# Eight PSUM banks, shared out anew: scores, transposes and products in a sliding-window attention block

## The chip, the cores and the metric

The kernel runs on one core of one Trainium2 chip, in one launch. The metric is the device time of that launch in microseconds. The engines are called by their short names: PE (TensorE, matmuls; PEld are its weight loads), DVE (VectorE), ACT (ScalarE), POOL (GpSimd) and SP (which here only starts DMAs). PSUM, into which PE writes, has eight banks of 128 x 512 floats; each PSUM tile of this kernel takes one bank.

## What is computed

A block with three residual steps on `x` of shape (8, 512, 512), float32: eight batch rows of 512 tokens. First and third come feed-forward steps, in the middle attention:

```python
x = x + 0.5 * ffn(layernorm(x), w_gate_up, w_proj)
x = x + attention(layernorm(x), Wq, Wk, Wv, Wo)
x = x + 0.5 * ffn(layernorm(x), w_gate_up, w_proj)
```

The attention has 32 heads of 16 values. A token sees itself and the 128 tokens before it, so a block of 128 queries needs its own block of keys and the previous one. Scores are `q k / 4`, then softmax, then the weighted sum of the values, then the output product with `Wo`. The feed-forward step has ternary weights, a gated SiLU and an RMS norm.

## The kernel before, in words

There are three stages: feed-forward "a", attention "b", feed-forward "c". Rows go between them through DRAM (`rows_a`, `rows_b`). The pools of a stage are laid out over the PSUM banks in the order in which they are opened, so attention reuses the banks of stage "a", and stage "c" those of attention. Stage "a" has its four accumulators first (`ps_acc`), then two gate-up banks (`ps_mm`), then two for transposes (`ps_tr`). Stage "c" opens its two transpose banks first, then four accumulators, then two gate-up banks.

In attention the work is cut into 128 **units** `u`. A head group `i = u // 4` holds eight of the 32 heads of one batch row (`i = 4 b + j`), and `t = u % 4` is the block of 128 tokens. In the text, `g` counts the four pairs of heads in a group; PE works on the four pairs side by side, each in 32 of its rows. For every unit there are:

- `maxima(u)` (L480, L489): scores with queries on the partitions, four tiles `sm`, one for each `g`. DVE masks each and takes its maximum into `negs`. It runs six units ahead (`AHEAD`).
- `subtract(i)` (L498, L501): after the four units of a head group, `negs` is transposed (`neg`) and the maxima are added into the queries as an extra component.
- `probabilities(u)` (L512 to L532): scores again with keys on the partitions, four tiles `sp`. ACT reads tiles g = 0, 2 and 3 (L525), DVE tile g = 1 (L521), both into `pT`; ACT then takes the exponential (L527), and POOL cuts off what lies outside the window (L532).
- `weighted(u)` (L548): values times `pT`, into `av`. After every second unit ACT copies it to `ab` (L557).
- `turned(u)` (L566): transposes `ab` into `abT`, for every second unit. `divided(u)` (L572, L576): DVE divides by the sum of the weights. `turned_back(u)` (L588, L591): transposes the result back, tile `oTp`, and ACT copies it to `oT`.

Between them lie the products with full-size matrices, one in each unit of a head group: values `wv` at t = 0 (read out by DVE), output `wo` of the previous row at t = 1 (DVE), queries `wq` at t = 2 (ACT, two copies), keys `wk` at t = 3 (ACT). All go through `sum_of_products` (L426). In the third head group of a row the layer norm of a later row is worked in: DVE scales (`xn_b`, L197), PE transposes (`ptn_b`, L205), ACT copies to `xs_b` (L213).

The order on PE, DVE, ACT and POOL inside this stage is the order in which the loop at the end of `attention_stage` calls these functions; the scheduler doesn't change it. It does merge that order with the instructions of the stages before and after. The first units have negative numbers: there row 0's norm (at high priority), the first products and the first maxima run. Units from 128 on (`units`) do what is left over, the output products of row 7 among them. A PSUM tile can be written as soon as its bank's last tile has been read out, and each engine works strictly in its order, so a tile without a bank holds up all of PE behind it.

Of the kernel before, what the change touches and what calls it, by code (L numbers as in the profile page):

```python
# [8 lines left out]
F32 = mybir.dt.float32  # L9
# [6 lines left out]
P = 128  # L16
# [8 lines left out]
def macaron_block(  # L25
# [20 lines left out]
    B, T, D = x.shape  # L46
    FF = w_proj.shape[1]
    TB, DC, FC = T // P, D // P, FF // P
# [50 lines left out]
    PSUM = bass.MemoryType.PSUM  # L99

    def pool(stack, name, bufs, space=bass.MemoryType.SB):

        return stack.enter_context(
            tc.tile_pool(name=name, bufs=bufs, space=space, reuse_waits="tile")
        )
# [64 lines left out]
    def inv_sqrt(dst, src):  # L170
        nc.gpsimd.tensor_tensor(dst, src, mhalf, ALU.pow)

    def norm(xnpool, xspool, psum, tag, xt, split, name):

        if split:
            xs = xspool.tile([P, 2, DC, T], F32R, tag="xs", name=f"xs_{name}")
        else:
            xs = xspool.tile([P, DC, T], F32, tag="xs", name=f"xs_{name}")  # L180
        mv = small.tile([P, TB, 2], F32, tag="mv", name=f"mv_{name}")
        rstd = small.tile([P, TB], F32, tag="nrstd", name=f"rstd_{name}")

        def statistics(t):
            st = small.tile([P, 6], F32, tag="st", name=f"st_{name}_{t}")
            nc.vector.bn_stats(st, xt[:, t, :])
            nc.vector.bn_aggr(mv[:, t, :], st)
            if t == TB - 1:
                var = small.tile([P, TB], F32, tag="nvar", name=f"var_{name}")
                nc.vector.tensor_scalar(var, mv[:, :, 1], LN_EPS, None, ALU.add)  # L190
                inv_sqrt(rstd, var)

        xns = {}

        def scaled(t):
            xns[t] = xnpool.tile([P, D], F32, tag="xn", name=f"xn_{name}_{t}")
            nc.vector.tensor_scalar(  # L197
                xns[t], xt[:, t, :], mv[:, t, 0:1], rstd[:, t : t + 1], ALU.subtract, ALU.mult
            )

        def transposed(t):
            xn = xns.pop(t)
            pt = psum.tile([P, DC, P], F32, tag=tag, name=f"ptn_{name}_{t}")
            for c in range(DC):
                nc.tensor.transpose(pt[:, c, :], xn[:, c * P : (c + 1) * P], ident)  # L205
            cols = slice(t * P, (t + 1) * P)
            if split:
                nc.scalar.copy(xs[:, 0, :, cols], pt)
                nc.vector.tensor_tensor(
                    xs[:, 1, :, cols], pt, xs[:, 0, :, cols].bitcast(F32), ALU.subtract  # L210
                )
            else:
                nc.scalar.copy(xs[:, :, cols], pt)  # L213

        return xs, statistics, scaled, transposed
# [155 lines left out]
    def attention_stage():  # L371
# [5 lines left out]
        s = ExitStack()  # L377
        xpool = pool(s, "x_b", 2)
        xspool = pool(s, "xs_b", 2)
        xnpool = pool(s, "xn_b", 2)  # L380
# [5 lines left out]
        probs = pool(s, "probs_b", 3)  # L386
        opool = pool(s, "o_b", 8)
        work = pool(s, "work_b", 3)
        ps_s = pool(s, "ps_s", 5, PSUM)
        ps_av = pool(s, "ps_av", 1, PSUM)  # L390
        ps_mm = pool(s, "ps_mm_b", 2, PSUM)

        xss, norms = {}, {}

        def row_loaded(b):
            xt = xpool.tile([P, TB, D], F32, tag="x", name=f"x_b{b}")
            nc.sync.dma_start(xt, rows_a[b])
            xss[b], *norms[b] = norm(xnpool, xspool, ps_mm, "mm", xt, False, f"b{b}")

        row_loaded(0)  # L400
        attn_w = {}
# [14 lines left out]
        abTs, qs, ks, kz, pTs, avs, abs_, os_, oTs = {}, {}, {}, {}, {}, {}, {}, {}, {}  # L416
        NJ = DC
        units = B * NJ * TB
# [2 lines left out]
            return u // TB // NJ, u // TB % NJ, u % TB  # L421

        def sum_of_products(name, pairs, done):
            ps = ps_mm.tile([P, T], F32, tag="mm", name=name)
            for n, (lhs, rhs) in enumerate(pairs):
                nc.tensor.matmul(ps, lhs, rhs, start=(n == 0), stop=(n == len(pairs) - 1))  # L426
            done(ps)
# [23 lines left out]
        def keys_of_head(i, h, kept, at):  # L451
            kz[i][h] = ring.tile([P, T], F32, tag=f"kz{h}", name=f"kz{h}_{i}")
            nc.gpsimd.tensor_scalar(kz[i][h], ks[i], kept, at, ALU.mult, ALU.add)
# [39 lines left out]
                    )  # L493

        def subtract(i):
            pt = ps_mm.tile([P, TB, P], F32, tag="mm", name=f"neg_{i}")
            for t in range(TB):
                nc.tensor.transpose(pt[:, t, :], negs[i % 2][:, t, :], ident)  # L498
            flat = pt.rearrange("p t q -> p (t q)")
            for h, at in enumerate((at16, at0)):  # L500
                nc.vector.scalar_tensor_tensor(qs[i][h], flat, at, qs[i][h], ALU.mult, ALU.add)  # L501
# [57 lines left out]
        def turned(u):  # L559

            i, t = u // TB, u % TB
            pt = abTs[i] = ps_mm.tile([P, 2, 2, P], F32, tag="mm", name=f"abT_{u}")
            ab = abs_.pop(i)
            for m in range(2):
                for h in range(2):
                    nc.tensor.transpose(pt[:, m, h, :], ab[:, h, m, :], ident)  # L566

        def divided(u):
            i, t = u // TB, u % TB
            rows = abTs.pop(i).rearrange("p m h (g r) -> p (m h) g r", r=32)  # L570
            rden = small.tile([P, 4, NG, 1], F32, tag="rden", name=f"rden_{u}")
            nc.vector.reciprocal(rden, rows[:, :, :, DK : DK + 1])  # L572
            os_[i] = work.tile([P, 2, NG, 2, DK], F32, tag="o", name=f"o_{u}", bufs=2)
            for m in range(2):
                for h in range(2):
                    nc.vector.tensor_tensor(  # L576
                        os_[i][:, m, :, h, :], rows[:, 2 * m + h, :, :DK],
                        rden[:, 2 * m + h].to_broadcast([P, NG, DK]), ALU.mult,
                    )

        def turned_back(u):
            i, t = u // TB, u % TB
            if t == 1:
                oTs[i] = opool.tile([P, T], F32, tag="oT", name=f"oT_{i}")
            o = os_.pop(i)
            back = ps_mm.tile([P, 2, P], F32, tag="mm", name=f"oTp_{u}")
            for m in range(2):
                nc.tensor.transpose(  # L588
                    back[:, m, :], o[:, m].rearrange("p g h d -> p (g h d)"), ident
                )  # L590
            nc.scalar.copy(  # L591
                oTs[i][:, (t - 1) * P : (t + 1) * P], back.rearrange("p m q -> p (m q)")
            )
# [23 lines left out]
        for u in range(-row - row // 2 - 2, units + row):  # L617
            i, t = u // TB, u % TB
            b, j = i // NJ, i % NJ
            if b == -2 and j == 2:  # L620
                with tc.high_priority():
                    if t == 0:
                        for block in range(TB):
                            norms[0][0](block)
                    for part in norms[0][1:]:
                        part(t)
            if 0 <= u < units:
                probabilities(u)
            if 0 <= u - 2 < units and (u - 2) % 2 == 1:
                divided(u - 2)  # L630
            if later:
                keys_of_head(*later.pop(0))
            if 0 <= u - 1 < units:
                weighted(u - 1)
            if t == 0 and 0 <= b - 1 < B:
                residual_loaded(b - 1, j)
            if 0 <= u + AHEAD < units:
                maxima(u + AHEAD)
            if j in (1, 2) and 0 < b + 2 < B:
                norms[b + 2][j - 1](t)  # L640

            if 0 <= u - 1 + AHEAD < units and (u - 1 + AHEAD) % TB == TB - 1:
                subtract((u - 1 + AHEAD) // TB)
            if b == -1 and j >= 2 and t < 2:
                values(0, 2 * (j - 2) + t)
            if t == 0 and 0 < b + 1 < B:
                values(b + 1, j)
            if t == 1 and 0 <= b - 1 < B:
                output(b - 1, j)
            if t == 2 and 0 <= i + 3 < B * NJ:  # L650
                queries(i + 3)
            if t == 3 and 0 <= i + 3 < B * NJ:
                keys(i + 3)
            if j == 2 and 0 < b + 2 < B:
                norms[b + 2][2](t)
            if 0 <= u - 1 < units and (u - 1) % 2 == 1:
                turned(u - 1)
            if 0 <= u - 2 < units and (u - 2) % 2 == 1:
                turned_back(u - 2)
            if j == 0 and t == 3 and 0 < b + 2 < B:  # L660
                row_loaded(b + 2)
# [33 lines left out]
```

## Time and profile before

| | us |
|---|---|
| median of 3 runs | 2562.67 (2561.23 to 2563.18) |
| profiled execution, its own time | 2563.55 |
| its span in the profile | 2561.5 |
| PE busy in the span | 2452.0 (96%) |
| DVE busy | 1310.7 (51%) |
| ACT busy | 977.0 (38%) |
| POOL busy | 948.5 (37%) |
| attention on PE, first `wq` to last `wo`, about | 831 to 1828 |
| PE, 1500 to 1600 us | busy 98.22 of 100 |

The page of the profile gives busy time by engine, then the chain of work that ended last, then the costliest groups of instructions. A timeline line reads: start, length, engine, line, operation, output <- inputs, sizes, how many, and in brackets how long the engine was idle before, and who ended the wait. Two things need care. A group's length on PE runs to the modelled end of its last matmul, which lies after the start of what follows; the time from start to start is the surer measure. And a group of matmuls that is held up in its middle counts as busy.

### The profile page before, as it was taken

Reading aid. Unit: us, or ns where it says so; the run is one execution under the profiler, and the core shown is the slowest. Engines: PE = TensorE matmul, PEld = TensorE weight load, DVE = VectorE, ACT = ScalarE, POOL = GpSimd, SP = SyncE. Lnnn points to the kernel's source line nnn. Section 1 sums busy time; section 2 is a strip of 40 time slices with the busy share of each in tenths; the row PEclk is TensorE's granted clock in tenths of the full one; section 3 lists DMA queues with packets and bytes.
Section 4 is the critical chain, followed back from the end, with each engine's and each line's share of the span. In section 5 each row is a group of like instructions: output and inputs, shape, how many; then the busy total and the mean of one; then the engine's idle time right before and its main releaser. Section 6 shows DMA issues by size and latency. Waiting matters only on the chain.

```text
span 2561.5 us, 40354 instructions
## 1 busy us (share of the span) xinstructions
PE 2452.0 (96%) x16184; PEld 1792.2 (70%) x16184; DVE 1310.7 (51%) x3785; ACT 977.0 (38%) x1460; POOL 948.5 (37%) x806
## 2 busy tenths in 40 slices
PE   5789999999999999999999999998999999999998
PEld 4668888888887555555555555555688888888887
DVE  7774434433434565666666565665334434443432
ACT  6662222222222355555555555555322222222221
POOL 0004444444445132333332332333244444444444
PEclk9899999999999999999999999999999999999999
DMA  4430000000011000101010000012400000000000
GB/s 156 140 132 33 34 17 17 33 33 1 34 66 66 34 1 28 36 18 34 22 34 18 18 22 18 19 62 105 144 1 33 33 33 1 34 33 1 34 17 17
DMA packets 38908, 103.26 MB, mean 40 GB/s; under 512 B 2880, under 2 KB 6976, under 8 KB 35648
## 3 DMA queue, kind: packets, MB, share of 16 engines
q1 hardware_dynamic: 28736, 75.51, 8.3%
q10 hardware_dynamic: 9984, 25.17, 2.9%
q8 instruction: 127, 2.08, 0.3%
q14 instruction: 61, 0.50, 0.1%
HBM read 62.91 MB, written 37.75 MB: 39 GB/s over the span
## 4 chain that ended last, share of the span: by engine, by line
PE 88%; DVE 7%; ACT 3%; issue 1%; DMA 1%; POOL 0%; DVEq 0%; POOLq 0%; ACTq 0%; SPq 0%
PE gu_a L233 18%; PE gu_c L233 18%; PE o_c L266 8%; PE o_a L266 8%; PE sm L480 6%; PE sp L512 5%; PE wk L426 5%; PE av L548 4%; PE wq L426 4%; PE wo L426 4%; PE wv L426 4%; PE abT L566 1%; DVE seen L489 1%; PE neg L498 1%; PE oTp L588 1%
## 5 line engine op out<-in xcount | busy, mean ns | idle before, releaser
L233 PE MATMUL gu_a<-xs_a,wgu_a 128*128 128x512 f32 x2048 | 506.9, 400 | 15.2 <-ACT wgu_a L153 15.2
L233 PE MATMUL gu_c<-xs_c,wgu_c 128*128 128x512 f32 x2048 | 488.8, 391 | 0.2 <-ACT sg_c L239 0.2
L532 POOL TENSOR_SCALAR_AFFINE_SELECT pT<-pT 128x1024 f32<-128x1024 f32 x224 | 241.7, 1099 | 630.3 <-ACT pT L527 629.3
L233 PEld LDWEIGHTS gu_a<-xs_a,wgu_a 128*128 128x128 f32 x2048 | 391.1, 193 | 98.9 <-ACT wgu_a L153 17.6
L233 PEld LDWEIGHTS gu_c<-xs_c,wgu_c 128*128 128x128 f32 x2048 | 382.9, 188 | 79.3 <-ACT sg_c L239 0.6
L489 DVE CUSTOM_DVE_ANT_0 seen<-sm,window 128x256 f32<-128x256 f32 (+1 forms) x1024 | 331.6, 388 | 107.5 <-PE sm L480 106.5
L266 PE MATMUL o_a<-wp_a,hs_a 128*128 128x512 f32 x1024 | 253.9, 391 | 5.9 <-ACT wp_a L153 5.9
L266 PE MATMUL o_c<-wp_c,hs_c 128*128 128x512 f32 x1024 | 251.5, 389 | 0.0
L259 POOL TENSOR_TENSOR sq_c<-h_c 128x512 f32<-128x512 f32 x120 | 125.0, 1042 | 323.0 <-DVE h_c L241 308.2
L241 DVE TENSOR_TENSOR h_c<-gu_c,sg_c 128x512 f32<-128x512 f32 x128 | 88.4, 691 | 292.4 <-PE gu_c L233 290.9
L525 ACT ACTIVATE pT<-sp 128x512 f32<-128x512 f32 (+1 forms) x384 | 181.1, 545 | 149.1 <-PE sp L512 148.5
L266 PEld LDWEIGHTS o_a<-wp_a,hs_a 128*128 128x128 f32 x1024 | 191.0, 188 | 46.8 <-ACT wp_a L153 7.8
L241 DVE TENSOR_TENSOR h_a<-gu_a,sg_a 128x512 f32<-128x512 f32 x128 | 88.4, 691 | 257.8 <-PE gu_a L233 256.4
L527 ACT ACTIVATE pT<-pT 128x2048 f32<-128x2048 f32 (+1 forms) x128 | 217.2, 1697 | 7.9 <-DVE var_c L190 2.1
L266 PEld LDWEIGHTS o_c<-wp_c,hs_c 128*128 128x128 f32 x1024 | 192.2, 188 | 39.9
L259 POOL TENSOR_TENSOR sq_a<-h_a 128x512 f32<-128x512 f32 x105 | 109.9, 1046 | 276.2 <-DVE h_a L241 264.8
L260 POOL TENSOR_TENSOR ss_c<-ss_c,sq_c 128x512 f32<-128x512 f32 x120 | 191.8, 1598 | 8.9
L521 DVE TENSOR_SCALAR pT<-sp 128x512 f32<-128x512 f32 (+1 forms) x128 | 80.0, 625 | 210.6 <-PE sp L512 202.1
L239 ACT ACTIVATE sg_c<-gu_c 128x512 f32<-128x512 f32 x128 | 76.7, 599 | 268.8 <-PE gu_c L233 268.8
L243 ACT CAST hs_c<-h_c 128x512 fp32r<-128x512 f32 x128 | 79.5, 621 | 257.0 <-DVE h_c L241 257.0
L239 ACT ACTIVATE sg_a<-gu_a 128x512 f32<-128x512 f32 x128 | 76.7, 599 | 258.3 <-PE gu_a L233 258.3
L480 PE MATMUL sm<-k,q 32*128 32x256 f32 (+1 forms) x2048 | 171.1, 380 | 3.2 <-DVE pT L521 1.6
(128 smaller groups left out, 3076.0 us busy)
## 6 DMA issues: line engine op xcount, KB each, us to landing
x_a<-x_dram SPq DMA_DIRECT2D x8, 1024.0 KB, 5.4
wf_gu<-w_gate_up_dram SPq DMA_DIRECT2D x16, 512.0 KB, 3.7
wgu_kept<-wgu_a SPq DMA_DIRECT2D x16, 512.0 KB, 2.8
rows_a<-x_a ACTq DMA_DIRECT2D x8, 1024.0 KB, 3.9
x_b<-rows_a SPq DMA_DIRECT2D x8, 1024.0 KB, 4.9
xr<-rows_a ACTq DMA_DIRECT2D x32, 256.0 KB, 3.1
rows_b<-xr SPq DMA_DIRECT2D x32, 256.0 KB, 2.4
x_c<-rows_b SPq DMA_DIRECT2D x8, 1024.0 KB, 4.8
```

Source lines behind the costliest of these rows:

```text
L233: nc.tensor.matmul(ps, wgu[c][:, i * DC + k, :], xs[:, s, k, :], start=(k == 0 and s == 0), stop=(k == DC - 1 and s == 1),)
L239: nc.scalar.activation(sg, gu[0], AF.Silu)
L241: nc.vector.tensor_tensor(h, gu[1], sg, ALU.mult)
L259: nc.gpsimd.tensor_tensor(sq, h, h, ALU.mult)
L260: nc.gpsimd.tensor_tensor(sumsq, sumsq, sq, ALU.add)
L266: nc.tensor.matmul(ops[t], ht[:, s, t * P : (t + 1) * P], wp[e // 2][:, e % 2, :], start=(e == 0 and s == 0), stop=(e == FC - 1 and s == 1),)
L426: nc.tensor.matmul(ps, lhs, rhs, start=(n == 0), stop=(n == len(pairs) - 1))
L480: nc.tensor.matmul(tiles[g][:, h, : n * P], qs[i][h][r, t * P : (t + 1) * P], ks[i][r, at], start=True, stop=True,)
L489: nc.vector.tensor_tensor_reduce(out=seen[:, : n * P], in0=tiles[g][:, h, : n * P], in1=window[:, (2 - n) * P :], scale=-1.0, scalar=3.4e3 ...
L525: nc.scalar.activation(under, tiles[g][:, :, : n * P], AF.Relu, scale=-1.0)
L527: nc.scalar.activation(seen, seen, AF.Exp, scale=-1.0)
L532: nc.gpsimd.affine_select(out=half, in_=half, compare_op=ALU.is_ge, fill=0.0, base=0, pattern=[[0, 2 * NG], [sign, P]], channel_multiplier ...
```

## The change

The score pool grows from five buffers to six. The product pool shrinks from two to one. The transposes (`ptn_b`, `neg`, `abT`, `oTp`) no longer use the product pool; they take buffers of the score pool, under its tag, in turn with the scores. The products take the one product buffer while `0 <= u < 128`, and score buffers before and after that. The division of a pair of units is called at the end of the unit that turned it, in place of the next unit, after that unit's `probabilities`. Nothing is computed otherwise.

```diff
-        ps_s = pool(s, "ps_s", 5, PSUM)
+        ps_s = pool(s, "ps_s", 6, PSUM)
         ps_av = pool(s, "ps_av", 1, PSUM)
-        ps_mm = pool(s, "ps_mm_b", 2, PSUM)
+        ps_mm = pool(s, "ps_mm_b", 1, PSUM)
...
-            xss[b], *norms[b] = norm(xnpool, xspool, ps_mm, "mm", xt, False, f"b{b}")
+            xss[b], *norms[b] = norm(xnpool, xspool, ps_s, "s", xt, False, f"b{b}")
...
         def sum_of_products(name, pairs, done):
-            ps = ps_mm.tile([P, T], F32, tag="mm", name=name)
+            space, tag = (ps_mm, "mm") if 0 <= u < units else (ps_s, "s")
+            ps = space.tile([P, T], F32, tag=tag, name=name)
...
         def subtract(i):
-            pt = ps_mm.tile([P, TB, P], F32, tag="mm", name=f"neg_{i}")
+            pt = ps_s.tile([P, TB, P], F32, tag="s", name=f"neg_{i}")
...
-            pt = abTs[i] = ps_mm.tile([P, 2, 2, P], F32, tag="mm", name=f"abT_{u}")
+            pt = abTs[i] = ps_s.tile([P, 2, 2, P], F32, tag="s", name=f"abT_{u}")
...
-            back = ps_mm.tile([P, 2, P], F32, tag="mm", name=f"oTp_{u}")
+            back = ps_s.tile([P, 2, P], F32, tag="s", name=f"oTp_{u}")
...
             if 0 <= u < units:
                 probabilities(u)
-            if 0 <= u - 2 < units and (u - 2) % 2 == 1:
-                divided(u - 2)
...
             if 0 <= u - 1 < units and (u - 1) % 2 == 1:
                 turned(u - 1)
+                divided(u - 1)
```

## The prediction

> **What bounds the kernel now.** I read the page first: busy time by engine, then the chain that ended last.
>
> ```profile
> PE 2452.0 (96%) x16184; PEld 1792.2 (70%) x16184; DVE 1310.7 (51%) x3785; ACT 977.0 (38%) x1460; POOL 948.5 (37%) x806
> PE 88%; DVE 7%; ACT 3%; issue 1%; DMA 1%; POOL 0%; DVEq 0%; POOLq 0%; ACTq 0%; SPq 0%
> ```
>
> TensorE is the bound, and the two feed-forward stages, untouched but for their borders, take all but about 980 us (831 to 1813). Inside attention, the view of waits (TensorE and its weight loads, 900 to 1780 us) looks harmless:
>
> ```profile
> PE abT L566 <- ACT ab L557: 6.8, 4, 1.8
> PE sm L480 <- DVE pT L521: 1.6, 1, 1.6
> PEld sm L480 <- DVE pT L521: 10.3, 44, 1.8
> ```
>
> The third line is the hint: the weight load of the score matmuls waits 44 times for an eviction. It hides in "busy" time, because some of the four matmul groups are already running. The timeline of TensorE shows it. One head group `i` is four units (t = 0 to 3):
>
> ```profile
> 998.76 1.15 PE L512 MATMUL sp<-q,kz 32*128 32x256 f32 x16
> 999.84 0.64 PE L548 MATMUL av<-pT,vones_sb 128*32 128x128 f32 x16
> 1000.41 1.83 PE L480 MATMUL sm<-k,q 32*128 32x256 f32 x16
> 1002.18 3.70 PE L426 MATMUL wo<-wo_sb,oT 128*128 128x512 f32 x8
> ...
> 1008.11 0.98 PE L480 MATMUL sm<-k,q 32*128 32x128 f32 x16
> 1009.02 0.66 PE L498 MATMUL neg<-ident,negs 128*128 128x128 f32 x4
> ...
> 1015.15 1.15 PE L480 MATMUL sm<-k,q 32*128 32x256 f32 x16
> 1016.23 3.70 PE L426 MATMUL wk<-xs_b,wk_sb 128*128 128x512 f32 x8
> ...
> 1022.16 1.40 PE L480 MATMUL sm<-k,q 32*128 32x256 f32 x16
> 1023.49 3.70 PE L426 MATMUL wv<-wv_sb,xs_b 128*128 128x512 f32 x8
> ```
>
> Start to start, `sm` takes 1.08 us at t=3, but 1.77 at t=1 and 1.33 at t=0. The half-width `sm` at t=2 takes 0.91, against 0.65 for a half-width `sp` (1013.49 to 1014.14). So 0.69 + 0.25 + 0.26 = **1.20 us of hidden stall** per `i`; a period is 28.80 us (994.69 to 1023.49). What `sm` waits for is in the all-engine timeline:
>
> ```profile
> 999.98 1.57 ACT L525 ACTIVATE pT<-sp 128x512 f32<-128x512 f32 x3 [3.49 <-PE sp L512]
> 1000.07 0.69 DVE L521 TENSOR_SCALAR pT<-sp 128x512 f32<-128x512 f32 x1 [0.94 <-PE sp L512]
> 1000.68 0.25 DVE L572 RECIPROCAL rden<-abT 128x16 f32<-128x16 f32 x1
> 1000.96 0.62 DVE L576 TENSOR_TENSOR o<-abT,rden 128x64 f32<-128x64 f32 x4
> ```
>
> With five buffers, the four `sm` tiles take one spare and those of `sp` g0 (ACT, 1000.58), g1 (DVE, 1000.76) and g2 (ACT's second, about 1001.07). The fourth group then needs its 1.07 us: 1001.12 + 1.07 = 1002.19, and `wo` starts at 1002.18. The model of the stall closes.
>
> **What the Trainium skill says.** "Perfetto Trace Analysis", Optimization Strategy: the same gap repeating on the engine that should be saturated can mean too few PSUM buffers. The trace agrees (every `i`). "PSUM — Partial Sum Buffer", Terms: eight banks. 5+1+2 and 6+1+1 both use all eight, so a score buffer is bought with a product buffer. "TensorE: Matmul & The Clock Gate", What's actually happening: after about 3.4 us of idling the array's clock halves until it has been busy about as long. The trace agrees: after 3.86 us idle at 945.5, `sp` took 2.02 us to the next start instead of 1.08, and the following `av` 1.50 instead of 1.01.
>
> **Part by part.** I read slots as a ring: a tile waits for the tile six (was five) before it. I choose this reading because the arithmetic above fits it.
>
> *Six buffers, transposes among them.* In order, an `i` takes: t=0 sp4, sm4, abT; t=1 sp4, sm4, oTp; t=2 sp4, sm4, neg, abT; t=3 sp4, sm4, oTp. Counting back six, `sm` now takes the last `sm` tile's slot, one transpose's slot, and `sp` g0 and g1. It no longer needs g2.
> - t=0: g1 is out at 1022.07, before `sm` starts at 1022.16. The stall of 0.25 goes.
> - t=2: g1 is out at 1007.99, `sm` starts 1008.11. The 0.26 goes.
> - t=1: `av` is only half as long here, so g1 (1000.76 + 0.05) still comes late: end 1000.81 + 1.07 = 1001.88 instead of 1002.18. Gain 0.30; 0.39 stays.
> - t=3: no stall before. After: `neg`'s, `abT`'s, g0's and g1's slots are free by about 1015.1 against a need from 1015.15 on. Nothing.
>
> Sum 0.81 per `i`. `sp` needs tiles of the previous unit's `sm`, read out by 1004.7 for a start at 1006.03: hidden. What is late next is g1's eviction by DVE at t=1.
>
> *The division moves.* The same five DVE instructions (0.25 + 0.62, about 0.9 us with the gap) now stand ahead of `pT` instead of behind it. `abT` ends 998.76 and DVE is done with `vones` at 999.12, so they fit into 999.14 to 1000.04, while DVE waits for `sp` until 1000.07: cost nothing, and `abT`'s slot is free 1.5 us earlier than today. At t=2/3 `abT` ends 1013.49, division to 1014.6, `pT` to 1015.0, needed at 1015.35: covered. Without that cover, g1 would be later by the whole 0.9.
>
> *One product buffer.* Each product must be read out before the next begins. wv: out 999.12, wo starts 1002.18. wo: 1006.60, wq 1009.52. wq: two ACT copies (0.69 + 0.68) to 1014.42, wk 1016.23. wk: 1020.56, wv 1023.49. The least slack is 1.8 us: cost nothing.
>
> *Norm transposes off the product buffers.* In the six rows with them, abT at t=2 waits for wq's copies through its buffer ("0.92 <-ACT q L440" at 1314.15), oTp at t=3 for wk's (0.24 shown, 0.3 by starts). Both go: 1.3 us. But at t=0 and t=1 `ptn_b` waits for DVE's `xn_b`, which follows `seen` and doesn't come earlier: of 0.25 + 0.30 only some 0.2 stays. Net about 0.9 beyond a plain `i`.
>
> *Sum inside.* Rows 1 to 6: 24 × 0.81 = 19.4. Norm extra in rows 1 to 5: 5 × 0.9 = 4.5. Row 0 has no `wo`, and its `sp` at t=2 waits for DVE's maxima: about 0.7 × 4 = 2.8. Row 7 waits at `abT` for ACT (1.6 to 3.1 us each), which swallows t=0 and t=2: 1. Gain **27.7 us**. Bounds: 15 (half of it swallowed by DVE) to 39 (t=1 wholly cured).
>
> *The entry.* Today row 0's four `ptn_b` run at 805.6 in the middle of the last feed-forward row, in banks that it has free; they cost 3.63 us there (16 gate-up matmuls take 801.12 to 808.38, 7.26 instead of 3.63). Now they start in the score buffers, whose first four banks are that stage's accumulators.
>
> ```profile
> 830.16 0.95 PE L274 MATMUL ms_a<-ones,ss_a 128*128 128x1 f32 x8
> 830.97 3.68 PE L426 MATMUL wq<-xs_b,wq_sb 128*128 128x512 f32 x8
> 832.64 2.73 DVE L284 SCALAR_TENSOR_TENSOR x_a<-o_a,half_a,x_a 128x512 f32<-128x512 f32 x4
> ```
>
> They must follow `x_a` (2.2 us after `ms_a` ends, all four by 4.3), then the third and fourth `xn_b` (0.55 each, two buffers), `ptn_b` and ACT's copy (0.6 + 0.6): `wq` starts about 6.7 us after `ms_a` instead of at once. Minus 3.63, minus the 0.35 stall at 842.3, plus 1.7 for a slow clock after that idling: **+4.4**, bounds 0 and +9.
>
> *The exit.* Today `ptn_c` fills a hole from 1806.96 while ACT and POOL finish the last `pT`. Its two banks now hold the last `abT` and the first late `wo` (final reads about 1814.9 and 1817.7). So some 2.5 us of transposes move out of the hole; the last `abT` and `wo` come forward by 1.3. **+1**, bounds −1 and +4. DMAs: none added, and SP's queue keeps its order.
>
> Total −27.7 + 4.4 + 1 = **−22.3**. The profiled execution took 2563.55 us (span 2561.5), 0.88 above the median of 2562.67. 2563.55 − 22.3 = 2541.2, or 2540.4 against the median.
>
> **Rivals.**
> - *As worked out*: 2540, own range 2527 to 2553. 0.76.
> - *DVE is the next gate*: the eviction of g1 and the maxima set the pace, so inside only 15 comes, and the borders cost 9 + 2: 2559, no change. For it: `seen` is 2.8 us per unit, and t=1 already hangs on g1. Against it: DVE is 18 of 28.8 us busy. 0.10, partly faster.
> - *The transposes' slots hold up the scores*: if the division runs after `pT` after all, or DVE is late by as much, `abT`'s slot is freed at 1001.58 instead of 1000.04, and `sm` at t=1 ends at 1001.58 + 0.06 + 1.07 = 1002.71, 0.53 worse than today; likewise t=3. Per `i` +1.05 − 0.51 = +0.54, × 31 + 5.4 = +22: 2585. It decides against the change from about 1001.2 on, that is 1.2 us later than I forecast. Against it: the division is issued ahead of `pT`. 0.10.
> - *The ring isn't a ring*, or the stall is ACT's pace and g1 as late as g2: t=1 gains nothing, −9.3: 2550. 0.04.
>
> **How the numbers follow.** A measurement of this kernel tells about 0.2% (5 us) from no change. Faster by more: the first case nearly whole, the last, some of the second: 0.82. Within: 0.08. Slower: 0.10. The range reaches from 2525 (t=1 wholly cured) to 2560, which takes in the second case and leaves the slow one out.
>
> **What would show it.** `sm` start to start: 1.08 at t=0, about 1.45 at t=1, 0.65 at t=2; period 28.0. Division before `pT` on DVE. "abT <- ACT q" gone. First `wq` about 6.7 us after `ms_a`, `ptn_b` between. Wrong: `sm` at t=1 or t=3 longer than before, a product waiting for `vones`, `q` or `k`, or an entry over 10 us.

## The result, and the profile after

The changed kernel took **2534.21 us** (median of four runs, 2530.88 to 2537.88) against 2562.93 in the runs of the kernel before beside it: ratio **0.989, 95% interval 0.987 to 0.991**. The forecast was 2540.4 with a range of 2525 to 2560. The profiled execution took 2530.88 us (span 2528.8), 32.7 less than the profiled one of before. In the listing of the changed kernel most lines of the attention stage stand two further down (`sm` is L482, `sp` L514, `pT` L523 and L527).

The page of the changed kernel: busy time by engine, then the chain that ended last.

```profile
PE 2421.7 (96%) x16184; PEld 1770.2 (70%) x16184; DVE 1304.7 (52%) x3785; ACT 974.9 (39%) x1460; POOL 946.9 (37%) x806
PE 89%; DVE 6%; ACT 2%; issue 1%; DMA 1%; POOL 0%; DVEq 0%; POOLq 0%; ACTq 0%; SPq 0%
```

PE does the same 16184 matmuls, is as full as before (96%), and is "busy" for 30.3 us less. That is how a stall inside matmul groups looks when it goes: the busy time shrinks, the share stays. The timeline of PE over one plain head group of the changed kernel shows where:

```profile
1333.43 3.70 PE L428 MATMUL wv<-wv_sb,xs_b 128*128 128x512 f32 x8
...
1339.15 1.53 PE L482 MATMUL sm<-k,q 32*128 32x256 f32 x16
1340.61 3.70 PE L428 MATMUL wo<-wo_sb,oT 128*128 128x512 f32 x8
...
1346.54 0.73 PE L482 MATMUL sm<-k,q 32*128 32x128 f32 x16
1347.20 0.66 PE L500 MATMUL neg<-ident,negs 128*128 128x128 f32 x4
...
1360.34 1.15 PE L482 MATMUL sm<-k,q 32*128 32x256 f32 x16
1361.41 1.12 PE L428 MATMUL wv<-wv_sb,xs_b 128*128 128x512 f32 x2
```

Start to start, `sm` takes 1.46 us at t=1 (was 1.77), 0.66 at t=2 (0.91) and 1.07 at t=0 (1.33); from `wv` to `wv` it is 27.98 us instead of 28.80. What is left at t=1 is in the all-engine timeline a head group later:

```profile
1365.76 0.25 DVE L574 RECIPROCAL rden<-abT 128x16 f32<-128x16 f32 x1
1366.04 0.62 DVE L578 TENSOR_TENSOR o<-abT,rden 128x64 f32<-128x64 f32 x4
1366.70 1.57 ACT L527 ACTIVATE pT<-sp 128x512 f32<-128x512 f32 x3 [3.24 <-PE sp L514]
1366.79 0.69 DVE L523 TENSOR_SCALAR pT<-sp 128x512 f32<-128x512 f32 x1
1367.13 1.53 PE L482 MATMUL sm<-k,q 32*128 32x256 f32 x16
1368.59 0.30 PEld L428 LDWEIGHTS wo<-wo_sb,oT 128*128 128x128 f32 x2 [0.33 <-issue]
```

The division now stands ahead of DVE's `pT`, which ends at 1367.48. Add 0.05 for the release and 1.07 for the fourth group, and `wo` starts at 1368.60; it started at 1368.59. The gate has moved from ACT's second tile to DVE's one, as worked out.

**Where the time went.** The span cut at four marks (the last `ms_a`, which ends stage "a" on PE; first `sp`; last `sp`; end), in us. The third row, first to last `sp`, is called "inside" below:

| | before | after | difference |
|---|---|---|---|
| start to last `ms_a` | 830.16 | 822.38 | −7.78 |
| last `ms_a` to first `sp` | 44.90 | 54.55 | +9.65 |
| first `sp` to last `sp` | 930.38 | 889.60 | −40.78 |
| last `sp` to end | 756.06 | 762.27 | +6.21 |
| span | 2561.5 | 2528.8 | −32.7 |

Of the first row, 3.63 us are the `ptn_b` that left the feed-forward row. The other 4.15 have nothing to do with the change: they are there long before any changed instruction, for the `ms_a` of the second row already stands at 279.07 us instead of 283.21. The start of the first stage varies: two kernels below with the same entry (e4 and e8) reach the last `ms_a` at 826.29 and 831.42. So the profiled difference overstates the change by about 4 us; the medians differ by 28.7.

The entry, in the chain of waits of the changed kernel (start, length, step):

```profile
823.61 1.02 POOL rms_a L171
...
824.86 2.73 DVE x_a L284 x4
827.58 0.47 DVE xn_b L197
828.05 0.04 issue
828.09 1.98 PE ptn_b L205 x8
...
830.10 0.59 ACT xs_b L213
830.69 0.04 issue
830.74 6.38 PE wq L428 x8
```

In the kernel before, PE went straight from `ms_a` to `wq`. Now the end of stage "a" and row 0's norm stand in between, one after the other, and `wq` then runs slowly (6.22 us to `wk` instead of 3.51): the clock granted to PE in the record is 0.50 of full speed from 825.9 to 836.2 us, where before it was 1.00 at the same place. The exit, on PE's timeline, first of before and then of the changed kernel:

```profile
1806.96 1.09 PE L205 MATMUL ptn_c<-ident,xn_c 128*128 128x128 f32 x8 [0.23 <-ACT pT L525]
...
1813.35 3.60 PE L426 MATMUL wo<-wo_sb,oT 128*128 128x512 f32 x8
...
1828.04 1.04 PE L205 MATMUL ptn_c<-ident,xn_c 128*128 128x128 f32 x8
1828.83 3.89 PE L233 MATMUL gu_c<-xs_c,wgu_c 128*128 128x512 f32 x16
```

```profile
1770.57 0.86 PE L550 MATMUL av<-pT,vones_sb 128*32 128x128 f32 x24 [1.58 <-POOL pT L534]
1772.14 1.11 PE L568 MATMUL abT<-ident,ab 128*128 128x128 f32 x4 [0.71 <-ACT ab L559]
1773.04 6.19 PE L428 MATMUL wo<-wo_sb,oT 128*128 128x512 f32 x8
...
1789.59 1.04 PE L205 MATMUL ptn_c<-ident,xn_c 128*128 128x128 f32 x8
1792.45 1.22 PE L205 MATMUL ptn_c<-ident,xn_c 128*128 128x128 f32 x8 [1.82 <-DVE xs_c L209]
1794.35 0.73 PE L233 MATMUL gu_c<-xs_c,wgu_c 128*128 128x512 f32 x2 [0.68 <-ACT xs_c L208]
```

The hole ahead of the last `av` is empty, and `ptn_c`, which filled it before, stands behind all four late `wo`, with its waits in the open. The first late `wo` runs at a granted clock of 0.50, too (1771.4 to 1778.3 us).

### The profile page after: what moved, and what is told of

Its sections match the earlier page's. It is cut to its first block, busy times and chain, and to the rows that moved or that the text cites. A ratio compares the mean times of both kernels' runs of the same rounds, so it can differ in the third digit from the quotient of the medians.

```text
span 2528.8 us, 40454 instructions
## 1 busy us (share of the span) xinstructions
PE 2421.7 (96%) x16184; PEld 1770.2 (70%) x16184; DVE 1304.7 (52%) x3785; ACT 974.9 (39%) x1460; POOL 946.9 (37%) x806
## 4 chain that ended last, share of the span: by engine, by line
PE 89%; DVE 6%; ACT 2%; issue 1%; DMA 1%; POOL 0%; DVEq 0%; POOLq 0%; ACTq 0%; SPq 0%
PE gu_c L233 18%; PE gu_a L233 18%; PE o_c L266 9%; PE o_a L266 8%; PE sm L482 5%; PE sp L514 5%; PE wk L428 5%; PE av L550 4%; PE wq L428 4%; PE wo L428 4%; PE wv L428 4%; PE abT L568 1%; PE neg L500 1%; PE ptn_b L205 1%; PE oTp L590 1%
## 5 line engine op out<-in xcount | busy, mean ns | idle before, releaser
L527 ACT ACTIVATE pT<-sp 128x512 f32<-128x512 f32 (+1 forms) x384 | 181.1, 547 | 129.4 <-PE sp L514 129.4
L260 POOL TENSOR_TENSOR ss_a<-ss_a,sq_a 128x512 f32<-128x512 f32 x105 | 167.6, 1596 | 7.8
L243 ACT CAST hs_a<-h_a 128x512 fp32r<-128x512 f32 x128 | 79.7, 622 | 227.0 <-DVE h_a L241 227.0
```

Source lines behind the costliest of these rows:

```text
L243: nc.scalar.copy(hs[c][:, 0, :], h)
L260: nc.gpsimd.tensor_tensor(sumsq, sumsq, sq, ALU.add)
L527: nc.scalar.activation(under, tiles[g][:, :, : n * P], AF.Relu, scale=-1.0)
```

## The experiments

They ask four things: is it the order of the division (e1, e7), the sixth buffer (e2, e5) or the separate product buffer (e6) that pays; is DVE's early release of g1 needed (e3); what do entry and exit cost (e4, e8); and is there a version that keeps the gain and pays no border (e9, e10). "Plain" and "norm" are the periods of a plain head group and of one with a layer norm: 28.80 and 33.39 us before, 27.98 and 30.43 after.

### e1: the division late again

```diff
             if 0 <= u < units:
                 probabilities(u)
+            if 0 <= u - 2 < units and (u - 2) % 2 == 1:
+                divided(u - 2)
...
                 turned(u - 1)
-                divided(u - 1)
```

> The changed kernel with one part undone: the division goes back to its old place, after the next unit's probabilities. Theory (a score tile waits for the tile six before it, abT's slot among these): the division ends about 1.5 us later, abT's slot is freed about 1.16 us after sp ends at t=1, and the second of the four sm groups waits for it. sm at t=1 then takes 2.3 us from start to start instead of 1.46, at t=3 about 1.6 instead of 1.08; a plain head group takes about 29.3 us (before the change 28.80, with it 27.98). Whole kernel 2570 to 2585 us, slower than before. Rival (six buffers give enough room whatever the order on DVE): 27.98 per head group stays, about 2534 us.

Measured: 2543.38, ratio to before 0.993 (0.991 to 0.996). Plain 28.29, norm 31.28. The all-engine timeline at a t=1:

```profile
1143.00 1.57 ACT L527 ACTIVATE pT<-sp 128x512 f32<-128x512 f32 x3 [3.24 <-PE sp L514]
...
1143.43 1.83 PE L482 MATMUL sm<-k,q 32*128 32x256 f32 x16
...
1143.97 0.62 DVE L578 TENSOR_TENSOR o<-abT,rden 128x64 f32<-128x64 f32 x4
...
1145.19 0.30 PEld L428 LDWEIGHTS wo<-wo_sb,oT 128*128 128x128 f32 x2 [0.33 <-issue]
```

The division ends at 1144.59. Had `sm` needed `abT`'s buffer, `wo` would have started at 1144.59 + 0.06 + 1.07 = 1145.72. It started at 1145.19, which fits ACT's second tile, read out at about 1144.09. That fits a late buffer being passed over for the next one to come free; it is read from these times, and not shown apart from them. The other units show no stall. The order of the division is worth 0.31 us per plain and 0.85 per norm head group, no more, and the price of the slow rival was wrong.

### e2: the new order and the sharing, with five and two buffers

```diff
-        ps_s = pool(s, "ps_s", 6, PSUM)
+        ps_s = pool(s, "ps_s", 5, PSUM)
-        ps_mm = pool(s, "ps_mm_b", 1, PSUM)
+        ps_mm = pool(s, "ps_mm_b", 2, PSUM)
...
-            xss[b], *norms[b] = norm(xnpool, xspool, ps_s, "s", xt, False, f"b{b}")
+            where = (ps_s, "s") if b > 1 else (ps_mm, "mm")
+            xss[b], *norms[b] = norm(xnpool, xspool, *where, xt, False, f"b{b}")
...
-            space, tag = (ps_mm, "mm") if 0 <= u < units else (ps_s, "s")
+            space, tag = ps_mm, "mm"
```

> The changed kernel's order and its transposes in the score rotation, but five score buffers and two product buffers as before; row 0's norm and all products stay in the product buffers, so that entry and exit are those of before. Theory (it is the sixth buffer that lets sm go without the eviction of sp g2): a plain head group stays at 28.8 us; only head groups with a norm gain, by 2.0 to 2.5 us instead of 2.97, as abT no longer waits for the two copies of wq. Whole kernel about 2550 us (5 x 2.2 + 2 below before). Rival (the gain comes from taking the transposes off the product buffers): plain head groups at 28.0 us and 2525 us, better than the change itself since the entry isn't paid.

Measured: 2563.43, ratio 1.0008 (1.0001 to 1.0014). Plain 28.80 as expected; norm 33.08, a gain of 0.31 where 2 and more were expected. In the norm head groups the wait only moves: `sm` is as short there as after the change at t = 0 and 2 (1.08 and 0.66 us), but the four `sp` together take 6.22 us from start to start where they took 3.89 before. A new wait appears once in each of six norm head groups, in the view of waits:

```profile
PE sp L515 <- ACT xs_b L213: 3.2, 6, 0.5
```

With five buffers `sp` now waits for the copy that frees `ptn_b`'s buffer. So moving the transposes gives next to nothing without the sixth buffer.

### e3: DVE takes g2, ACT takes g1

```diff
-                if g == 1:
+                if g == 2:
                     nc.vector.tensor_scalar(
```

> The changed kernel with one digit changed: DVE reads tile g = 2 of sp in place of g = 1, ACT reads 0, 1 and 3. Same instructions, same lengths, same number on each engine. Theory (with six buffers sm waits for g0 and g1, so what counts is that these two are evicted by two engines): now g1 is ACT's second eviction, 0.3 us later, and the stalls of before come back: sm 1.33 at t=0, 1.77 at t=1, 0.91 at t=2, 28.8 us for a plain head group; norm head groups keep most of their gain. Whole kernel about 2556 us. Rival (six buffers give room, who evicts which tile is of no account): 27.98 us and about 2534 us.

Measured: 2561.27, ratio 0.9996 (0.9988 to 1.0005). Plain 28.80 as expected: `sm` takes 1.33, 1.77 and 0.91 us at t = 0, 1, 2, the stalls of before to the hundredth. Norm 31.54. With six buffers `sm` still needs the first two `sp` tiles, and the second is now ACT's second. So the buffer alone gives nothing in a plain head group either: it pays because the second tile is read out by the other engine, beside the first. The forecast of 2556 for the whole kernel was missed: inside is 917.00, 13.4 less than before, mostly in the rows with a norm, but the two borders cost 10.7 of it here, and the median comes out as before.

### e7: the division alone, in the kernel before

```diff
                 probabilities(u)
-            if 0 <= u - 2 < units and (u - 2) % 2 == 1:
-                divided(u - 2)
...
                 turned(u - 1)
+                divided(u - 1)
```

> The kernel before with one part of the change: the division is called at the end of the unit that turned it; buffers as before. Theory (the order on DVE is worth something only together with the sixth buffer, since sm waits for ACT's eviction of g2): a plain head group stays at 28.8 us; in the norm head groups xn_b at t=1 starts earlier, which gives 0.4 to 0.6 us each. Whole kernel 2558 to 2561 us, 0 to 4 below before. Rival (DVE's order alone carries the gain): 28.5 us per head group, 2552 us.

Measured: 2562.71, ratio 1.0007 (0.9998 to 1.0015); plain 28.8, norm 33.39. No gain at all, in the norm head groups neither: there `xn_b` at t=1 takes 1.41 to 1.43 us as before.

### e6: the transposes through the one product buffer

The tiles `neg`, `abT` and `oTp` stay in the product pool, now of one buffer:

```diff
-            pt = ps_s.tile([P, TB, P], F32, tag="s", name=f"neg_{i}")
+            pt = ps_mm.tile([P, TB, P], F32, tag="mm", name=f"neg_{i}")
```

> The changed kernel, but abT, neg and oTp stay in the product pool, which has one buffer. Theory (a product's eviction is covered only as long as nothing follows it into its bank at once): abT waits for the copy of wv (about 0.9 us), oTp for that of wo (0.9), wq for the two uses of neg on DVE (2.6), abT for the two copies of wq (1.6), oTp for that of wk (0.8): 6.7 us per head group on top of 28, about 34.8 us, whole kernel 2720 to 2780 us. Rival (PE finds the time elsewhere, ACT and DVE are only half busy): below 2600 us.

Measured: 2796.6 (one run), plain about 37.2, where 34.8 was expected. The view of waits, 1000 to 1700 us (total, times, longest):

```profile
PE wq L428 <- DVE q L503: 58.6, 19, 3.8
PE abT L568 <- ACT q L442: 24.0, 19, 1.4
PE oTp L590 <- DVE xr L607: 12.4, 18, 0.8
```

`wq` waits until DVE has read `neg`, 3.1 us each on the mean, and after that idling it runs slowly (its group is 5.1 to 5.4 us long where 3.6 is usual). In one plain head group the five waits come to 6.45 us, close to the 6.7 expected; what the expectation left out is the slow `wq` (1.8); about 1 us of the 9.2 stays open. The transposes must leave the product pool when it has one buffer.

### e4: entry and exit out of the scores' buffers

Row 0's `ptn_b`, all products outside 0 ≤ u < 128, and the last `abT` and `oTp` take the product buffer and the one of `av` in turn:

```diff
+        class Borders:
+            turn = 0
+
+            def tile(self, shape, dtype, tag, name):
+                self.turn += 1
+                space, tag = ((ps_av, "av"), (ps_mm, "mm"))[self.turn % 2]
+                return space.tile(shape, dtype, tag=tag, name=name)
...
-            space, tag = (ps_mm, "mm") if 0 <= u < units else (ps_s, "s")
+            space, tag = (ps_mm, "mm") if 0 <= u < units else (borders, "s")
```

> The changed kernel with its two borders undone: row 0's norm transposes and all products before unit 0 and after unit 127 take the banks of av and of the products in turn (the two banks that the product pool had before), and so do the last abT and oTp. Between the borders nothing is changed. Theory (the entry costs 6 us net in the trace, the exit 4.5): row 0's ptn_b runs inside the last feed-forward row again, wq follows ms_a at once, ptn_c starts in the hole before the last av; the head groups stay at 27.98. Whole kernel 6 to 10 us below the changed kernel, 2524 to 2529 us. Rival (the waits at the borders are covered by other work, the time comes out the same): 2534 us.

Measured: 2523.09, ratio 0.985 (0.9835 to 0.9865). `wq` follows `ms_a` after 0.80 us again, last `ms_a` to first `sp` takes 44.25, inside 890.13 (unchanged), last `sp` to end 756.53. Both borders are back at the values of before. The exit on PE's timeline:

```profile
1764.19 1.47 PE L205 MATMUL ptn_c<-ident,xn_c 128*128 128x128 f32 x8
1765.59 0.86 PE L560 MATMUL av<-pT,vones_sb 128*32 128x128 f32 x24
...
1768.35 3.60 PE L438 MATMUL wo<-wo_sb,oT 128*128 128x512 f32 x8
```

`ptn_c` is in the hole ahead of the last `av`, and the first late `wo` runs at full speed.

### e8: only the entry out of them

As e4, with the last `abT`, `oTp` and `wo` left in the scores' buffers. Against the change:

```diff
-            xss[b], *norms[b] = norm(xnpool, xspool, ps_s, "s", xt, False, f"b{b}")
+            xss[b], *norms[b] = norm(xnpool, xspool, ps_s if b else borders, "s", xt, False, f"b{b}")
...
-            space, tag = (ps_mm, "mm") if 0 <= u < units else (ps_s, "s")
+            space, tag = (ps_mm, "mm") if 0 <= u < units else (ps_s if u > 0 else borders, "s")
```

> The changed kernel with only the entry undone: row 0's norm transposes and the products before unit 0 take the banks of av and of the products in turn. The exit is that of the change. Theory (entry and exit each cost, and add up): wq follows ms_a at once; 5 to 7 us below the changed kernel, about 2528 us, the rest of the gain of e4_borders (about 5) stays in the exit. Rival (all of e4's gain is the entry, the exit is hidden by the feed-forward stage's own wait): 2523 us.

Measured: 2534.24, ratio 0.990 (0.988 to 0.991); no better than the change, where 2528 was expected. The entry is cured (44.25), but last `sp` to end is 766.9, 4.6 more than after the change, and the last `ms_a` came late in this run (831.42). One line of PE's timeline names the new wait:

```profile
1791.74 1.09 PE L205 MATMUL ptn_c<-ident,xn_c 128*128 128x128 f32 x8 [2.34 <-DVE xr L617]
```

`ptn_c` now waits for the reading out of the last `wo`. Taking tiles out of a rotation at one end shifts which buffer every later tile gets, and here the last `wo` fell on one that stage "c" needs first. That it is the same buffer was read from the order of the tiles, and not tried by itself.

### e5: seven buffers for scores, transposes and products alike

```diff
-        ps_s = pool(s, "ps_s", 6, PSUM)
+        ps_s = pool(s, "ps_s", 7, PSUM)
-        ps_mm = pool(s, "ps_mm_b", 1, PSUM)
...
-            space, tag = (ps_mm, "mm") if 0 <= u < units else (ps_s, "s")
+            space, tag = ps_s, "s"
```

> The changed kernel with the last product buffer given to the scores too: seven buffers in one pool for scores, transposes and products (and one for av). Theory (at t=1 the last sm group waits for the eviction that frees the fourth slot; with seven it is sp g0, ACT's first, 0.17 us earlier than DVE's g1): sm at t=1 takes 1.30 us from start to start instead of 1.46, a plain head group 27.8 us instead of 27.98; t=0, 2 and 3 stay without a stall. Whole kernel about 2529 us with the borders unchanged, 5 us below the change. Rival (products hold their buffers too long for a shared pool): a head group of 28.5 us or more and 2545 us.

Measured: 2526.27, ratio 0.987 (0.9847 to 0.9892). Plain 27.80, norm 30.28, inside 882.99. PE's timeline at t=1:

```profile
1139.44 1.35 PE L481 MATMUL sm<-k,q 32*128 32x256 f32 x16
1140.72 3.70 PE L427 MATMUL wo<-wo_sb,oT 128*128 128x512 f32 x8
```

Of the 0.39 us of stall that the change leaves there, 0.18 go (1.28 us start to start); what ends the rest fits ACT's first tile, as expected: ACT starts on `sp` at 1139.01 and is done with its first tile about 0.60 later; with 0.05 and 1.07 more `wo` would start at 1140.73, and it starts at 1140.72.

### e9 and e10: seven buffers, borders elsewhere

e9 is e5 with row 0's norm and the first `wq` in the buffer of `av`. e10 is e9 with everything from unit 128 on, and the last `abT` and `oTp`, there too:

```diff
+            where = (ps_s, "s") if b else (ps_av, "av")
...
+            space, tag = (ps_av, "av") if name == "wq_0_0" or u >= units else (ps_s, "s")
...
+            space, tag = (ps_av, "av") if u == units - 1 else (ps_s, "s")
```

(In e9 the second line has no `or u >= units`, and the third is missing.)

> The kernel of e5 (seven shared buffers) with row 0's norm transposes and the first wq in the bank of av, which stage a has free, so that they run in the middle of the last feed-forward row. With these five tiles gone from the rotation, the last tiles fall on other banks: the first two transposes of stage c find oTp of unit 125 and the last abT ahead of them, not the last output product. Theory (inside, entry and exit are independent terms): a plain head group 27.8 us, wq straight after ms_a, ptn_c no later than the last abT; 5 to 9 us below e5, 2517 to 2521 us, the fastest of all. Rival (one bank for row 0's four transposes makes them wait for each other in the feed-forward row and costs there what it saves at the border): about 2526 us.

> Seven shared buffers as in e5, the entry's tiles as in e9, and beside them everything from unit 128 on (the last wo's, and the last abT and oTp) in the one buffer of the value products. Theory: ptn_c is held up only when a late tile stands in the scores' rotation; with none there the exit runs as in e4 (last sp to first gu_c about 23.6 us, against 27.4 in e9), inside as e5 (first to last sp about 883), so 2517 to 2520 us, ratio about .983, ptn_c before the last wo. Rival: the last four wo and abT share one buffer, each waits some .9 us for the eviction of the one before it, and that eats the gain: last sp to first gu_c stays at 26 to 28 us and the time at 2522 to 2524.

Measured: e9 2522.91, ratio 0.985 (0.983 to 0.987); e10 2522.30, ratio 0.984 (0.983 to 0.986). Entry (44.29 in both) and inside (883.14 and 883.31) are as expected. The exit is not, and both miss their forecasts (2517 to 2521 and 2517 to 2520): last `sp` to end is 763.86 in e9 and 761.5 in e10, against 756.53 in e4. PE's timeline of e10:

```profile
1763.66 0.63 PE L205 MATMUL ptn_c<-ident,xn_c 128*128 128x128 f32 x4 [0.56 <-DVE xs_c L209]
...
1768.16 3.67 PE L428 MATMUL wo<-wo_sb,oT 128*128 128x512 f32 x8 [0.66 <-DVE o L579]
...
1773.71 3.70 PE L428 MATMUL wo<-wo_sb,oT 128*128 128x512 f32 x8 [0.65 <-ACT oT L595]
1778.90 3.70 PE L428 MATMUL wo<-wo_sb,oT 128*128 128x512 f32 x8 [1.49 <-DVE xr L609]
1783.39 3.70 PE L428 MATMUL wo<-wo_sb,oT 128*128 128x512 f32 x8 [0.78 <-DVE xr L609]
```

In e9, with the late tiles in the scores' rotation, `ptn_c` comes behind the last `wo`, at 1780.22. In e10, with none of them there, it is back ahead of the first: that part of the theory holds. But the late tiles now share one buffer: the first late `wo` waits for the division of `abT` in it (0.66 us) and starts 10.1 us after the last `sp`, against 7.7 in e4, and two others wait 2.27 us together for the `wo` before to be read out: the rival's mechanism, and its time. With its last `ms_a` as early as e4's, e10 would be about 2 us ahead of e4 (`ms_a` to end 1689.1 against 1690.9), which is less than these runs tell apart. e4, e9 and e10 all beat the change by some 11 us, and none of the three is shown to be the best.

## Why the prediction was right, point by point

- **The hidden stall, and its cure by the sixth buffer: right to 0.01 us.** 0.81 was worked out per plain head group, 0.82 measured, with the forecast values at t = 0, 1 and 2. e2 and e3 show that both halves are needed: without the sixth buffer, or with g1 read out by ACT, the period is 28.80 again.
- **The division: right in place, mis-priced as a risk.** It runs in DVE's free time. But I read the buffers as a strict ring, and the times of e1 fit a buffer that comes free late being passed over. The case that I had priced at 2585, the division after `pT`, came out at 2543 in e1: 9 us above the change, and still faster than before. The 0.10 that I gave to "slower" rested on it for the most part.
- **One product buffer: right.** No wait of a product for `vones`, `q` or `k` shows inside. e6 shows what protects it: only products use it.
- **Norm head groups: the term of 0.9 was too small.** They gained 2.97, that is 2.16 beyond a plain one (mean of five), so 6.3 us were missed, 1.26 per norm head group. From start to start it can be seen where. The waits of `abT` on ACT's `q` and of `oTp` on ACT's `k` are gone, as forecast, and gave 1.59 instead of 1.3. At t=0 and t=1 I had let 0.35 of the plain gain be lost; 0.55 was gained on top of it. About half of that difference of 0.9 is a term that I left out: `abT` at t=0 and `oTp` at t=1 had also waited for DVE to read out `wv` and `wo`, and now follow `ptn_b` 0.24 and 0.17 sooner (before, DVE was done with `wv` at 1296.68 and `abT` started at 1296.83; with `wo` at 1305.28, and `oTp` started at 1305.34). The other half is a step that failed, "doesn't come earlier" for `xn_b`: at t=1 `ptn_b` now starts 3.54 us after `wo` instead of 3.94. In e3, where `xn_b` is as late as before, that time is 4.03, and the norm head groups still gain 1.85. All-engine timeline, first of before and then of after, at t=1 of the same norm head group:

```profile
1302.26 2.15 POOL L532 TENSOR_SCALAR_AFFINE_SELECT pT<-pT 128x1024 f32<-128x1024 f32 x2 [5.55 <-ACT pT L527]
1303.25 1.43 DVE L197 TENSOR_SCALAR xn_b<-x_b,mv_b,rstd_b 128x512 f32<-128x512 f32 x1
```

```profile
1285.09 2.32 POOL L534 TENSOR_SCALAR_AFFINE_SELECT pT<-pT 128x1024 f32<-128x1024 f32 x2 [5.37 <-ACT pT L529]
1285.79 0.68 DVE L197 TENSOR_SCALAR xn_b<-x_b,mv_b,rstd_b 128x512 f32<-128x512 f32 x1
```

  Alone `xn_b` takes 0.54 us. Before, it starts 0.99 us after POOL's first select, and ends 0.27 us after the second. After, it starts 0.70 us in and ends between the two, and the pair of selects takes 2.32 instead of 2.15. The Trainium skill, "SBUF — State Buffer", Who interferes with whom, says that DVE and POOL share a pair of ports, that `tensor_scalar` can be among the operations that take it, and that the one that issues first holds it for its whole instruction while the other waits. The traces agree, with e1, e2, e3 and e7 too: there `xn_b` starts 0.99 to 1.02 us in and takes 1.40 to 1.43. In e5 it starts 0.70 to 0.71 in and takes 0.67 to 0.68. The lock itself was not tried by an experiment of its own.
- **Row 0 and row 7: 2.8 and 1 forecast, 6.0 and 3.6 measured.** Row 0's third head group is also one with a norm, which the term left out, and gained 2.1; its first gained 2.4, where 0.7 had been put down for each. Why the first did, and what row 7 gained by, stays open. Rows 1 to 6 gained 31.2 where 23.9 were forecast, so inside came to 40.8 instead of 27.7.
- **The entry: +4.4 forecast, +6.0 measured** (9.65 less the 3.63 that left the row before). `wq` started 7.4 us after the last `ms_a` ended, not 6.7, and its slow clock cost 2.7, not 1.7. e4 shows that all of it is the choice of buffer.
- **The exit: +1 forecast, with 4 as its upper bound; +6.2 measured.** The step that failed is that the two transposes would move only behind the first late `wo`. They came behind all four. To the first `gu_c` this makes 4.4 us (27.82 after the last `sp`, against 23.39): the chain of `ptn_c` behind the last `wo` takes 4.8 us (1789.59 to 1794.35) where 0.8 stood before, the first late `wo` takes 6.03 us to the next start instead of 3.44, and the places where `ptn_c` stood before give 2.1 back. Another 1.0 is lost to the transposes that now stand between the first `gu_c`, and 0.8 later in stage "c", which stays open. e4 undoes it; e4 against e8, with one entry and two exits (756.53 and 766.9), and e10 against e9 tie the place of `ptn_c` to the late tiles' buffers.

So the sum inside was 13 us too low, and the two borders 6.8 us too cheap. Against the profiled execution, −40.8 + 6.0 + 6.2 − 4.15 makes −32.7. That the forecast lay only 6 us from the median is partly such errors cancelling; the side and the mechanism were right.

## What to carry to other kernels

Busy time hides a stall for buffers inside a matmul group, so compare the time from start to start of the same group at different places. When a buffer is added, ask who reads out the tile that is needed next: a sixth buffer was worth nothing until that tile belonged to the other engine. And look at the two ends of a stage whose buffers its neighbours reuse: here the borders cost 12 us of a gain of 41, and keeping a few tiles out of the rotation gave 11 back.

## What the hardware showed that I had not expected

- A matmul group runs slowly after less idling than I had reckoned with. "TensorE: Matmul & The Clock Gate", What's actually happening, speaks of some 3.4 us of idling. In the granted clock of these records the fall from 1.00 to 0.50 comes sooner. At the new entry it is at 825.9 us, after a single idle time of 2.34 us (and the one-column matmuls of `ms_a` before that). In e6 it is at 1043.1, after one of 2.74, and even in the example of my prediction (before, 941.7 to 945.5) the clock falls at 943.3, some 1.6 us into the idle time. The length of one idle time does not decide it either: at the exit 3.11 us of idling before 1765.94 leave the clock at 1.00, and the fall comes at 1771.4, after another 1.58. Here the measurements decide against the figure; what rule they follow is not shown.
- A DVE scaling that takes 0.54 us alone takes 0.68 or 1.43 beside POOL's two selects at t=1: 0.68 when it starts 0.70 us after the first of them, 1.43 when it starts 0.3 us later.
